# Attention over a sparse graph on one core: gathered rows in a ring, one reduction for a tile's weighted sum, VectorE in the order of the program

## The chip, the cores and the metric

The kernel runs on one core of a Trainium2 chip. A core has five engines that run side by side, each with its own queue of instructions: TensorE (PE, matrix products), VectorE (DVE, elementwise operations and reductions), ScalarE (ACT, functions and copies), GpSimd (POOL, here above all the issuer of indirect DMAs) and SyncE (SP, an issuer of plain DMAs). Engines wait for one another through semaphores; transfers are made by 16 DMA engines. Each of the 128 partitions of on-chip memory (SBUF) holds one row of a tile; results of TensorE land in PSUM, eight banks of 512 float32 values a partition. The metric is the time of one execution on the device, in microseconds (us).

## The reference

There are 3327 nodes with 256 values each, and an adjacency matrix in which an entry is set with probability 0.0024 and the diagonal always. Four layers follow one another: an attention block, a layer that averages over neighbours, and two more attention blocks.

```python
def attention_block(x, adj, w_qkv, w_proj, b_proj, w1, b1, w2, b2, g1, be1, g2, be2):
    qkv = layer_norm(x, g1, be1) @ w_qkv          # 8 heads of 32
    q, k, v = ...
    scores = jnp.einsum('nhd,mhd->hnm', q, k) * SCALE
    scores = jnp.where(adj != 0, scores, -jnp.inf)
    attn = jax.nn.softmax(scores, axis=-1)
    out = jnp.einsum('hnm,mhd->nhd', attn, v).reshape(n, DIM)
    x = x + out @ w_proj + b_proj
    h2 = layer_norm(x, g2, be2)
    return x + jax.nn.gelu(h2 @ w1 + b1) @ w2 + b2    # 256 -> 1024 -> 256

def averaging(x, adj, Wt, bt, Wa, ba, Wp, bp, gamma, beta):
    h = x @ Wt.T + bt                              # 64 values
    s = leaky_relu(h @ Wa.T + ba, 0.2)
    w = softmax(where(adj > 0, s, NEG), axis=1)
    y = x + (w @ h) @ Wp.T + bp
    return layer_norm(y, gamma, beta)
```

## The kernel before

The first stage reads the adjacency matrix once and makes for each node a list of its neighbours, at most 24. Nodes are sorted by the number of neighbours and divided into 26 tiles of 128, a node to a partition. `ROOM[t]` is the number of neighbour rows that tile t needs: 24, 14, 12, 12, 11, 11, 10, 10, then 9 four times, down to 4; together 228. The normalised rows are multiplied with the key, value and query weights, and keys and values go to a table in device memory, 512 values a row.

An attention block (`block`, L634) processes the tiles from the last to the first, so that lists grow from 4 rows to 24, in groups of 2, 2, 3, 4, 4, 4, 3, 2, 1 and 1 tiles (`GROUPS`, L62). For each tile:

- `scores` (L551) loads the tile's own key, value, query row (and, in blocks 0 and 1, the residual x) into `own`: in block 0 by an indirect DMA of POOL (L559), in block 1 and 2 by SP (L564, L566). ACT copies x out of it (L568) and the query into a PSUM bank named `qs` (L571; two such banks). `gather` (L546) issues one indirect DMA on POOL for each neighbour index; it fetches 128 rows of 512 values. Four of them fill a unit; the pool has ten units. For the own row and each unit, VectorE multiplies the keys with the query in place (L576) and sums over each head's 32 values into the scores in PSUM (L577). Then empty places are pushed away (L591), the maximum is subtracted (L593, L595), and ACT takes the exponent (L596).
- `weighed` (L599), one tile later, divides by the sum (L605 to L607), multiplies the values with the weights (L610), and adds the units up: full units onto the first (L622), the partial one (L626), then halves onto halves (L630) and the own row last (L631).
- When a group is complete, `project` (L651 to L665) transposes the result and multiplies it with the projection's weights; the bias is a small matmul for each tile (`bias`, L187). Later steps of the loop (`run`, L720) add the residual and sum it up on the way (`add`, L667, VectorE's L671), normalise (`norm`, L205: squares on ACT, then a chain of some twelve tiny VectorE operations with `root`, L192), turn and feed forward (`feed_forward`: L685, the gelu on ACT at L688, the second matmul with result `f2` at L695), add again, and hand the rows on: block 0 to the averages (`into_averages`, L792), block 1 to the keys of block 2 (`into_keys`, L755), block 2 to the output by indirect DMAs (L711). A group's stages are held in the list `later`, each with the step from which it may run.

The order in which engines carry out their instructions is not the order in which the code emits them: the framework's scheduler lists all instructions of a stage and orders each engine by its own model of costs and by priorities, within what data and buffers allow. Only where `tc.manual_schedule(engines={...})` is entered does the named engine keep the order of the program; before, that is so for VectorE in a part of the adjacency stage only.

The averaging layer (`averaging`, L850) takes its buffers for turned adjacency (`at`) and for rows (`st4`) from the same pool of units.

Of the kernel before, what the change touches and what calls it, by code (L numbers as in the profile page):

```python
# [19 lines left out]
BF = mybir.dt.bfloat16  # L20
# [11 lines left out]
P = 128  # L32
CW = 512
# [26 lines left out]
UNIT = 4  # L60
UNITS = 10
# [20 lines left out]
def chunk_width(c):  # L82
    return min(CW, NP - c * CW)


class Sparse:
# [100 lines left out]
    def bias(self, y, i):  # L187

        self.nc.tensor.matmul(y, self.ones3, self.biases[:, i, :], start=True, stop=False)
# [15 lines left out]
    def norm(self, pool, tiles, sums):  # L205
# [6 lines left out]
        for i, t in enumerate(tiles):  # L212
            xh = pool.tile([P, DIM], F32, tag="xh", name="xh", bufs=2)
            nc.scalar.activation(xh, t, AF.Square, bias=m[:, i : i + 1], accum_out=v[:, i : i + 1])
        nc.vector.tensor_scalar(v[:, :n], v[:, :n], 1.0 / DIM, EPS, ALU.mult, ALU.add)
# [23 lines left out]
    def turned(self, pool, pp, tiles, gamma=None, beta=None, small=None, sums=None):  # L239
# [3 lines left out]
        if sums is not None:  # L243
            rstd, shift = self.norm(pool, tiles, sums)
        elif gamma is not None:
            _, rstd, shift = self.stats(pool, tiles, small)
# [297 lines left out]

    def gather(self, out, table, t, j, held):
# [6 lines left out]
    def scores(self, pool, pp, layer, t, held):  # L552

# [3 lines left out]
        own = pool.tile([P, 4 * DIM], F32, tag="own", name="own", bufs=3)  # L557
        if layer == 0:
# [3 lines left out]
            )  # L562
        elif layer == 1:
            self.after(nc.sync.dma_start(out=own, in_=self.sorted[ts(t, P), :]), self.turning)  # L564
        else:
            nc.sync.dma_start(out=own[:, : 3 * DIM], in_=self.own[t])  # L566
        if layer < 2:
            nc.scalar.copy(self.x[t], own[:, 3 * DIM :])  # L568
# [3 lines left out]
        s = bank[:, ds(DIM, (SLOTS + 1) * HEADS)].rearrange("p (j h) -> p j h", h=HEADS)  # L572
        units = []

        def dot(at, k, n):
            nc.vector.tensor_mul(k, k, query.unsqueeze(1).to_broadcast([P, n, DIM]))  # L576
            nc.vector.tensor_reduce(  # L577
                s[:, ds(at, n), :].rearrange("p j h -> p (j h)"), k.rearrange("p j (h d) -> p j h d", d=HD), AX.X,
                ALU.add,
            )  # L580

        dot(0, own[:, :DIM].unsqueeze(1), 1)
        for j0 in range(0, J, UNIT):
            n = min(UNIT, J - j0)
            u = self.units.tile([P, UNIT, 2 * DIM], F32, tag="unit", name="unit")
            for j in range(n):
                self.gather(u[:, j, :], self.places[layer], t, j0 + j, held)
            dot(1 + j0, u[:, :n, :DIM], n)
            units.append((u, j0, n))
        away = self.away[:, t, :J].unsqueeze(2).to_broadcast([P, J, HEADS])  # L590
        nc.vector.tensor_add(s[:, ds(1, J), :], s[:, ds(1, J), :], away)  # L591
        top = pool.tile([P, HEADS], F32, tag="top", name="top", bufs=3)
        nc.vector.tensor_reduce(top, s[:, : J + 1, :].rearrange("p j h -> p h j"), AX.X, ALU.max)  # L593
        wide = [P, J + 1, HEADS]
        nc.vector.tensor_sub(s[:, : J + 1, :], s[:, : J + 1, :], top.unsqueeze(1).to_broadcast(wide))  # L595
        nc.scalar.activation(s[:, : J + 1, :], s[:, : J + 1, :], AF.Exp)  # L596
        return own, s, units

    def weighed(self, pool, t, own, s, units):  # L599
# [3 lines left out]
        wide = [P, J + 1, HEADS]  # L603
        total = pool.tile([P, HEADS], F32, tag="total", name="total", bufs=3)
        nc.vector.tensor_reduce(total, s[:, : J + 1, :].rearrange("p j h -> p h j"), AX.X, ALU.add)  # L605
        nc.vector.reciprocal(total, total)
        nc.vector.tensor_mul(s[:, : J + 1, :], s[:, : J + 1, :], total.unsqueeze(1).to_broadcast(wide))  # L607

        def weigh(to, v, at, n):
# [971 lines left out]
```

## Time and profile before

| | |
|---|---|
| median of three runs | 2087.87 us (2083.0 to 2097.82) |
| the profiled execution | 2096.42 us |
| its span | 2094.6 us |
| granted clock of TensorE, mean | 0.77 |

| stage | from to, us | VectorE busy | TensorE busy |
|---|---|---|---|
| adjacency, neighbour lists, keys and values | 0 to 306 | | |
| attention block 0 | 306 to 850 | 367.0 | 311.2 |
| averaging | 850 to 1072 | 106.2 | 194.7 |
| attention block 1 | 1072 to 1604 | 356.5 | 367.2 |
| attention block 2 | 1604 to 2094 | 344.1 | 283.3 |

The span is the time from the first to the last instruction in the trace, all numbers in it are of one execution. A group of the profile reads: line, engine, operation, out<-in with their shapes, count, then busy time and mean of one, then the time for which the engine stood idle before them and what ended it. A wait reads: engine, the name and line of the instruction that waited, the instruction it waited for, then us in total, times, and the longest. A line of the timeline reads: start, duration, engine, line, operation; a count behind it, as x2, means that so many instructions are taken together. Waits are inferred from semaphores; busy time counts what overlaps on one engine once.

### The profile page before, as it was taken

What the parts mean: (1) busy time and instruction counts of PE and PEld (TensorE: products, weight loads), DVE (VectorE), ACT (ScalarE), POOL (GpSimd) and SP (SyncE); (2) the same over time, 40 slices, a digit from 0 to 9 for tenths busy, and PEclk for the clock granted to TensorE, in tenths of its full rate; (3) what the DMA queues carried; (4) which work ended last, traced back from release to release, by engine and by line L of the source; (5) the groups of instructions that cost most, each with busy time, mean ns of one, the idle gap of its engine ahead of it and who ended that gap; (6) DMA issues with size and microseconds to landing.
All of it is one profiled execution on the core that took longest, in us unless ns stands there. A gap on an engine that the chain in (4) does not pass through costs nothing. (4 is left out here: it accounts for less than half of the span.)

```text
span 2094.6 us, 17222 instructions
## 1 busy us (share of the span) xinstructions
PE 1263.4 (60%) x4806; PEld 812.1 (39%) x4806; DVE 1342.0 (64%) x3407; ACT 684.9 (33%) x1420; POOL 1001.0 (48%) x946
## 2 busy tenths in 40 slices
PE   3244411556755579699934688567695277655676
PEld 1122200344424337577512454343473154323445
DVE  3567635577776785165636789776732679976871
ACT  3555501233321224122322444334343133322232
POOL 3768757555555531101156645555203666565521
PEclk8667655677767769799976888798798587767778
DMA  8878827555555550858486656656215665565520
GB/s 191 330 300 326 284 79 213 160 163 154 170 148 175 147 131 23 198 154 230 160 284 205 216 166 209 220 178 193 61 56 201 210 186 176 176 190 160 152 65 20
DMA packets 169409, 369.73 MB, mean 177 GB/s; under 512 B 78821, under 2 KB 90291, under 8 KB 165976
## 3 DMA queue, kind: packets, MB, share of 16 engines
q0 software_dynamic: 68624, 222.01, 35.4%
q1 hardware_dynamic: 85689, 112.44, 17.1%
q10 hardware_dynamic: 14990, 34.08, 5.0%
q8 instruction: 40, 0.66, 0.1%
q14 instruction: 66, 0.54, 0.1%
HBM read 279.77 MB, written 77.59 MB: 171 GB/s over the span
## 5 line engine op out<-in xcount | busy, mean ns | idle before, releaser
L546 POOL DMA_INDIRECT unit<-kv,ids x684 | 667.2, 975 | 434.7 <-issue 189.1
L685 PE MATMUL f<-hT,w 128*128 128x256 f32 (+3 forms) x960 | 342.1, 517 | 58.6 <-ACT gT L688 23.2
L256 PE MATMUL tr<-ident,xh 128*128 128x128 f32 x312 | 80.6, 384 | 442.7 <-ACT xh L251 395.6
L695 PE MATMUL f<-w,gT 128*128 128x256 f32 x1248 | 306.4, 399 | 17.9 <-ACT gT L688 14.3
L685 PEld LDWEIGHTS f<-hT,w 128*128 128x128 f32 x960 | 190.4, 219 | 202.6 <-issue 106.0
L695 PEld LDWEIGHTS f<-w,gT 128*128 128x128 f32 x1248 | 238.3, 197 | 68.7 <-ACT gT L688 18.3
L256 PEld LDWEIGHTS tr<-ident,xh 128*128 128x128 f32 x312 | 41.7, 179 | 483.3 <-ACT xh L251 414.8
L576 DVE TENSOR_TENSOR unit<-unit,qs 128x1024 f32<-128x1024 f32 (+3 forms) x198 | 211.7, 1069 | 26.4 <-DMA unit<-kv,ids 15.0
L577 DVE TENSOR_REDUCE qs<-unit 128x32 f32<-128x1024 f32 (+3 forms) x198 | 212.7, 1074 | 4.8 <-DVE qs L607 1.7
L610 DVE TENSOR_TENSOR unit<-unit,qs 128x1024 f32<-128x1024 f32 (+3 forms) x198 | 210.0, 1065 | 0.0
L315 POOL TENSOR_TENSOR m<-a,place 128x3328 f16<-128x3328 fp8e4 x26 | 159.4, 6132 | 78.7 <-ACT a L313 78.6
L688 ACT ACTIVATE gT<-f,b 128x256 f32<-128x256 f32 (+3 forms) x240 | 124.8, 536 | 212.5 <-PE f L685 106.6
L538 PE MATMUL kvps<-wqkv,hT 128*128 128x512 f32 x312 | 171.9, 677 | 29.5 <-ACT hT L262 22.5
L326 DVE MAX8 found<-m 128x8 f16<-128x416 f16 x208 | 111.5, 579 | 39.7 <-POOL m L315 33.1
L664 PE MATMUL proj<-wproj,oT 128*128 128x256 f32 x312 | 109.3, 489 | 42.7 <-ACT oT L659 22.8
L576 DVE TENSOR_TENSOR own<-own,qs 128x256 f32<-128x256 f32 x78 | 32.3, 415 | 141.5 <-ACT qs L571 124.2
L658 PE MATMUL otr<-ident,o 128*128 128x128 f32 x156 | 25.5, 289 | 142.4 <-DVE qs L577 87.4
L990 POOL DMA_INDIRECT sorted<-st,to x26 | 24.8, 955 | 178.7 <-ACT st L542 147.1
L538 PEld LDWEIGHTS kvps<-wqkv,hT 128*128 128x128 f32 x312 | 63.2, 213 | 86.7 <-issue 37.7
L313 ACT ACTIVATE a<-a 128x3328 fp8e4<-128x3328 int32 x26 | 77.3, 2973 | 51.6 <-DMA kv<-st 29.0
L251 ACT ACTIVATE xh<-x,shift,rstd 128x256 f32<-128x256 f32 x104 | 58.4, 594 | 104.5 <-DVE shift L218 80.9
L664 PEld LDWEIGHTS proj<-wproj,oT 128*128 128x128 f32 x312 | 66.9, 235 | 65.6 <-ACT oT L659 28.4
(193 smaller groups left out, 1881.4 us busy)
## 6 DMA issues: line engine op xcount, KB each, us to landing
a<-in_adj SPq DMA_DIRECT2D x25, 1663.5 KB
kv<-st ACTq DMA_DIRECT2D x52, 512.0 KB
own<-sorted SPq DMA_DIRECT2D x26, 512.0 KB
unit<-kv,ids POOLq DMA_INDIRECT x684
adj<-a SPq DMA_DIRECT2D x26, 416.0 KB
own<-qkv SPq DMA_DIRECT2D x26, 384.0 KB
own<-own SPq DMA_DIRECT2D x26, 384.0 KB
w<-in_L_gnn_w SPq DMA_DIRECT2D x6, 1024.0 KB
```

What stands on the lines that cost most here:

```text
L256: nc.tensor.transpose(ps[k][:, ts(q, P)], t[:, ts(k, P)], self.ident)
L315: nc.gpsimd.tensor_mul(m.rearrange("p (s e) -> p s e", e=SEG), a8.rearrange("p (s e) -> p s e", e=SEG), place.unsqueeze(1).to_broadcast([P ...
L326: nc.vector.max(found[:, i, s, :], m[:, ts(s, SEG)])
L538: nc.tensor.matmul(kv, hT[:, k, ts(q, P)], w[:, k, DIM : 3 * DIM], start=k == 0, stop=k == KC - 1)
L546: g = self.nc.gpsimd.indirect_dma_start(out=out, out_offset=None, in_=table, in_offset=bass.IndirectOffsetOnAxis(ap=self.ids[:, t, j : j + ...
L576: nc.vector.tensor_mul(k, k, query.unsqueeze(1).to_broadcast([P, n, DIM]))
L577: nc.vector.tensor_reduce(s[:, ds(at, n), :].rearrange("p j h -> p (j h)"), k.rearrange("p j (h d) -> p j h d", d=HD), AX.X, ALU.add,)
L610: nc.vector.tensor_mul(to.rearrange("p j (h d) -> p j h d", d=HD), v.rearrange("p j (h d) -> p j h d", d=HD), s[:, ds(at, n), :].unsqueeze ...
L664: nc.tensor.matmul(y, oT[:, k, ts(q, P)], wpj[:, k, :], start=False, stop=k == KC - 1)
L685: nc.tensor.matmul(y[:, :w], w1[:, k, ts(f, P)], hT[:, k, :w], start=k == 0, stop=k == KC - 1)
L688: nc.scalar.activation(gT[-1][:, f % 2, :w], y[:, :w], AF.Gelu_apprx_tanh, bias=b1[:, f : f + 1])
L695: nc.tensor.matmul(y, gT[f // 2][:, f % 2, ts(q, P)], w2[:, f, :], start=False, stop=f == FC - 1)
```

## The change

- One tile `ring` of 46 rows takes the place of the ten units of four rows. `take(n)` hands out the next n rows and begins again at the front where they do not fit. A tile takes `ROOM[t]` + 2 rows: the neighbours first, and the tile's own row in the last two, beside them.
- `fetch` is split off `scores`: own row, gathers and the query's copy of a tile are issued after the weighing of the tile two before it, that is a tile ahead of its scores. x no longer passes over ACT; SP writes it by a DMA of its own.
- Products and weighing run over pieces of up to 6 (`PIECE`) and 9 (`WEIGHED`) rows, own row included. The sum over rows is one reduction for a tile that steps from row to row (L656 of the kernel after).
- VectorE keeps the program's order through a whole block.
- `norm` is split in `squares` (residual, sum, ACT's squares) and the rest; what follows waits in the list `middle` and is issued by `between` after the next tile's scores. The averages' preparation is split in the same way (`rest`, a stage of its own).
- The biases of two halves of a bank are one matmul; the flag that ends the accumulation is set once for a bank (`Halves`).

```diff
-UNIT = 4
-UNITS = 10
+RING = 46
+PIECE = 6
+WEIGHED = 9
...
-    def bias(self, y, i):
-        self.nc.tensor.matmul(y, self.ones3, self.biases[:, i, :], start=True, stop=False)
+    def bias(self, ys, q, i):
+        if q % 2 == 0:
+            bank, n = ys.bank(q)
+            self.nc.tensor.matmul(
+                bank[:, : n * DIM], self.ones3, self.biases[:, i, :].unsqueeze(1).to_broadcast([3, n, DIM]),
+                start=True, stop=False,
+            )
...
-    def norm(self, pool, tiles, sums):
+    def squares(self, pool, tiles, sums):
...
             nc.scalar.activation(xh, t, AF.Square, bias=m[:, i : i + 1], accum_out=v[:, i : i + 1])
+        return m, v
+
+    def norm(self, pool, n, m, v):
...
+    def take(self, n):
+        if self.at + n > RING:
+            self.at = 0
+        at = self.at
+        self.at += n
+        return self.ring[:, at : at + n, :]
...
-    def scores(self, pool, pp, layer, t, held):
+    def fetch(self, pp, layer, t, held):
         J = ROOM[t]
-        own = pool.tile([P, 4 * DIM], F32, tag="own", name="own", bufs=3)
+        rows = self.take(J + 2)
+        own = rows[:, J:, :].rearrange("p a b -> p (a b)")
         if layer == 0:
             nc.gpsimd.indirect_dma_start(
...
+            nc.sync.dma_start(out=self.x[t], in_=own[:, 3 * DIM :])
         elif layer == 1:
-            self.after(nc.sync.dma_start(out=own, in_=self.sorted[ts(t, P), :]), self.turning)
+            for to, at in ((own[:, : 3 * DIM], self.sorted[ts(t, P), : 3 * DIM]), (self.x[t], self.sorted[ts(t, P), 3 * DIM :])):
+                self.after(nc.sync.dma_start(out=to, in_=at), self.turning)
         else:
             nc.sync.dma_start(out=own[:, : 3 * DIM], in_=self.own[t])
-        if layer < 2:
-            nc.scalar.copy(self.x[t], own[:, 3 * DIM :])
+        for j in range(J):
+            self.gather(rows[:, j, :], self.places[layer], t, j, held)
         bank = pp.tile([P, CW], F32, tag="qs", name="qs", bufs=2)
         query = bank[:, :DIM]
         nc.scalar.copy(query, own[:, 2 * DIM : 3 * DIM])
+        return rows, bank
+
+    def scores(self, pool, t, rows, bank):
...
-        dot(0, own[:, :DIM].unsqueeze(1), 1)
-        for j0 in range(0, J, UNIT):
-            n = min(UNIT, J - j0)
-            u = self.units.tile([P, UNIT, 2 * DIM], F32, tag="unit", name="unit")
-            for j in range(n):
-                self.gather(u[:, j, :], self.places[layer], t, j0 + j, held)
-            dot(1 + j0, u[:, :n, :DIM], n)
-            units.append((u, j0, n))
+        for lo, w in self.pieces(n, PIECE):
+            k = rows[:, ds(lo, w), :DIM]
+            nc.vector.tensor_mul(k, k, query.unsqueeze(1).to_broadcast([P, w, DIM]))
+            nc.vector.tensor_reduce(
...
-        full = [u for u, _, n in units if n == UNIT]
-        for u in full[1:]:
-            nc.vector.tensor_add(full[0][:, :, DIM:], full[0][:, :, DIM:], u[:, :, DIM:])
...
-        nc.vector.tensor_add(o, o, u[:, 0, DIM:])
+        for lo, w in self.pieces(n, WEIGHED):
+            v = rows[:, ds(lo, w), DIM:].rearrange("p j (h d) -> p j h d", d=HD)
+            nc.vector.tensor_mul(v, v, s[:, ds(lo, w), :].unsqueeze(3).to_broadcast([P, w, HEADS, HD]))
+        o = pool.tile([P, DIM], F32, tag="o", name="o", bufs=5)
+        nc.vector.tensor_reduce(o, rows[:, :n, DIM:].rearrange("p j f -> p f j"), AX.X, ALU.add)
         return o
...
+            def forward(at, group, sums):
+                add_later(at + max(2, len(group)), 1, group, feed_forward(group, sums))
+            def follow(at, group, sums):
+                after, rest = finish(group, sums)
+                if rest:
+                    add_later(at + 1, 2, group, rest)
+                add_later(at + 1 + (len(group) > 2 or rest is not None), 3, group, after)
...
+                    if stage == 0:
+                        middle.append((forward, at, group, squares(group, what)))
+                    elif stage == 1:
...
+                            middle.append((follow, at, group, squares(group, what)))
...
+            with tc.manual_schedule(engines={nc.vector.engine}):
+                waiting, step, outs = None, 0, []
+                got = fetch()
+                for group in [*GROUPS, ()]:
+                    for t in group or (None,):
+                        now = t is not None and (group, t, *self.scores(pool, t, *got))
+                        between()
+                        if waiting:
+                            done, *rest = waiting
+                            outs.append(attended(*rest))
+                        got = fetch()
+                        if waiting and len(outs) == len(done):
+                            add_later(step + 1 + (len(done) > 2), 0, done, project(done, outs))
                             outs = []
+                        waiting = now
+                        run(step)
+                        step += 1
+                between()
+                run(None)
```

## The prediction

> **What bounds the kernel now.** I read the busy shares first, then the span by stage, then VectorE's waits, then the costs of single operations.
>
> ```profile
> PE 1263.4 (60%) x4806; PEld 812.1 (39%) x4806; DVE 1342.0 (64%) x3407; ACT 684.9 (33%) x1420; POOL 1001.0 (48%) x946
> ```
>
> No engine is full on average, so the stages decide. The windows view was asked for the steady middle and the tail of each attention block; its columns are the stretch, its length, then busy time of PE, PEld, DVE, ACT and POOL, the granted clock, DMA share and GB/s.
>
> ```profile
> 322.00:805.00 483.00, 274.44 (x939) 177.02 (x940) 348.24 (x756) 136.77 (x314) 252.91 (x260) 0.71 0.54 156
> 805.00:850.00 45.00, 36.80 (x213) 30.87 (x212) 13.22 (x67) 18.17 (x61) 10.73 (x12) 0.96 0.33 101
> ...
> 1084.00:1529.00 445.00, 299.38 (x957) 181.75 (x958) 341.94 (x751) 165.11 (x359) 229.78 (x233) 0.79 0.58 180
> 1529.00:1604.00 75.00, 67.80 (x300) 47.85 (x298) 13.62 (x81) 40.30 (x106) 9.62 (x10) 1.00 0.33 120
> 1622.00:2048.00 426.00, 251.59 (x825) 157.98 (x826) 335.37 (x711) 118.68 (x245) 235.39 (x239) 0.74 0.54 162
> 2048.00:2094.00 46.00, 31.22 (x172) 26.13 (x170) 4.62 (x27) 12.81 (x35) 5.73 (x6) 0.87 0.07 23
> ```
>
> In the three middles (1354 us together) DVE is the busiest engine: 1025.5 us busy, 328.5 us idle. Matrix work fills the tails. What DVE waits for in the first middle (total us, times, longest):
>
> ```profile
> DVE own L576 <- ACT qs L571: 38.8, 7, 14.8
> DVE total L605 <- ACT qs L596: 21.9, 5, 9.0
> DVE h L818 <- PE hps L810: 14.5, 5, 9.8
> ...
> DVE unit L576 <- DMA unit<-kv,ids: 9.0, 2, 7.7
> ```
>
> The largest is the first product of a tile, behind the copy of its query on ACT, which follows the load of the tile's own row; rows themselves are rarely awaited. So the change moves two quantities: DVE's work, which rises, and its 328.5 us of idling, which it can replace.
>
> **The change, part by part.** The costs come from VectorE's groups by form, and from its timeline in the averaging layer:
>
> ```profile
> L577 DVE TENSOR_REDUCE qs<-unit 128x32 f32<-128x1024 f32 x144 | 175.7, 1220 | 2.2 <-remote 1.6 <-DVE qs L607 0.5
> L576 DVE TENSOR_TENSOR unit<-unit,qs 128x1024 f32<-128x1024 f32 x144 | 174.8, 1214 | 24.4 <-DMA unit<-kv,ids 15.0 <-issue 7.9 <-DVE total L606 1.2
> ...
> L382 DVE TENSOR_REDUCE larger<-more 128x25 bf16<-128x650 f32 x1 | 1.3, 1317 | 0.0
> ...
> L442 DVE TENSOR_REDUCE count<-tops 128x26 f32<-128x624 f32 x1 | 0.8, 793 | 0.0
> ```
> ```profile
> 902.17 0.16 DVE L201 SCALAR_TENSOR_TENSOR nwt<-nwt,rstd 128x4 f32<-128x4 f32 x1
> 902.37 0.16 DVE L202 SCALAR_TENSOR_TENSOR rstd<-nwt,rstd 128x4 f32<-128x4 f32 x1
> ...
> 904.55 0.75 DVE L981 TENSOR_TENSOR st<-st,beta 128x256 f32<-128x256 f32 x2
> ```
>
> 1024 elements take about 1215 ns and 256 elements 415 ns (the same L576 on the own row), so an operation costs 147 ns and 1.04 ns an element. Two independent 417 ns operations of L981 fit in 0.75 us: the second starts 80 ns before the first ends. L202 needs L201's result and starts 40 ns after its end (34 ns by finer times). A pair in dependent order is thus 114 ns dearer than an independent one.
>
> *Products, scores and weighing.* A block has 228 gathered and 26 own rows. Before, 92 operations each for product, score sum and weighing (276); after, pieces of up to 6 and 9 rows make 54 + 54 + 39 = 147. The elements stay; 129 operations fewer save 147 - 80 = 67 ns each: **-8.6 us a block**.
>
> *The sum over neighbours.* Before, 118 contiguous additions (L622, L626, L630, L631) are 78.6 us busy a block, or 69.2 with the 80 ns of overlap taken off each. After, 26 reductions read 254 x 256 = 65,024 elements, each sum stepping over whole rows, 2048 bytes apart. No row of before has that stride. Lower end: contiguous reductions, L442 or L577, 1.04 ns an element, 69.5 us. L382 is the only large reduction with a stride, 100 bytes: (1317 - 147)/650 = 1.80 ns, 118.8 us. Upper end: twice 1.04, a slot lost on every element, 137 us. L382's lines are still packed closer than 2048 bytes, so I take 2.0 ns, near the upper end: 132 us, **+62.6 us a block**.
>
> The Trainium skill, "SBUF — State Buffer", section "Door 1: The DMA port swizzle (why `[64,N]` ≈ `[32,N]`)", says that SBUF is read in 16-byte lines, that full bandwidth needs two hits a line, and that four fp32 is as far as one strides for free. It speaks against this reduction, gives no factor, and would by itself rule out the lower end; L382 agrees, but is one row.
>
> *VectorE in the order of the program.* Before, the framework's scheduler interleaves tiles: in the middles 700, 676 and 655 pairs of neighbours overlap, and only 13, 24 and 9 start as dependent. In the program's order product, score sum and softmax steps follow their own producers: by the two orders 376, 396 and 316 pairs become dependent, x 114 ns = 43 + 45 + 36 = **+124 us for three blocks**. Upper end: all of it. Lower end nothing, if the chip treats wide operations otherwise than L201 and L202.
>
> The Trainium skill, "VectorE: DVE Perf Modes", section "The DRAIN you can't avoid", says that the next operation waits for the pipe anyway and that a semaphore between two costs nothing extra (8 copies in 13.88 us either way). By it these 124 us would be nothing and the sum about 2000; the trace's 0.75 us for two 0.417 us operations contradicts it, and I go by the trace.
>
> DVE's work thus changes by 3 x (62.6 - 8.6) + 124 = **+286 us** (+99 at 1.04 ns, +247 at 1.80, +302 at 2.08).
>
> *Fetch a tile ahead, own row in the ring, query copied at the fetch, norm in two steps.* Own row and query copy are now issued before the weighing of the previous tile is consumed, so L571's wait should go, and the norm's squares on ACT run beside the next tile's scores. That takes away most of the 328.5 us. What comes late next, by the program's fixed order:
> - Groups of two tiles: the second matmul's result f2 is due two steps on. Tile chains of 6 to 10 rows cover 17 to 19 us, while such a feed-forward takes 22 to 26 (squares at 1668.8, last f2 at 1694.7). Behind that wait stand add, squares and the next scores. About 12 us a block.
> - The ring has 46 rows. The three largest tiles (24 + 2, 14 + 2, 12 + 2) overlay the tile but one before, whose rows come free only when its whole sum has ended. Then own row, gathers at 1.25 us each and landing (3.9 us in the chain) come late. About 15 us a block.
> - First gathers and the averages' split step: about 8.
>
> So new waits S of 33 to 37 us a block, some 100 in all, against 328.5: **-228**. Lower bound nothing; upper bound the old waits.
>
> *POOL.* Its gathers start 1.25 us apart:
>
> ```profile
> 1640.64 0.95 POOL L546 DMA_INDIRECT unit<-kv,ids  x1 [0.30 <-issue]
> 1641.89 0.95 POOL L546 DMA_INDIRECT unit<-kv,ids  x1 [0.31 <-issue]
> ```
>
> With own rows (block 0) and scatters that is 350, 317 and 317 us a block, under DVE's about 430 to 470 after, so DVE hides it. If the stride were free, DVE would shrink to about 375 + waits and POOL's order would matter.
>
> *Smaller parts.* One bias matmul for two halves: 52 to 60 fewer small matmuls a block on a PE that has slack in the middles; it counts in the tails. The copy of x moves from ACT to SP's queue: one DMA more per tile in blocks 0 and 1, behind loads of the same queue; ACT, 28 to 37% busy, loses 0.4 us a tile. The x rows are needed only at the projection a tile or more later, so nothing; without that cover some 2 us a tile. Averaging takes the same buffers from the ring: nothing, or a few us either way. In the tails the last groups end sooner because the norm no longer waits its turn among the scheduler's choices: 5 to 8 us each, -20 in all, from the 166 us of the three tails; bounds 0 and -40.
>
> **Sum.** +286 - 228 - 20 = +38. The profiled execution took 2096.42 us, 8.5 above the median 2087.87; the sum is made of the profiled execution's durations and applied to the median: 2126, given as **2125 us** (2134 against the profiled execution).
>
> **Rivals.** (A) The forecast, DVE-bound with a stride near 2 ns: 2085 (1.80 ns, S = 35) to 2165 (2.08 ns, S = 45), chance 0.45.
>
> (B) The fixed order exposes more: each DVE wait now holds everything behind it, where the scheduler could pass another tile's work. For it: L605, L671 and L818 waits on ACT and PE are already there, and PE at .71 to .79 clock is 57 to 67% busy in the middles. Against: products of a later tile stand between most producers and consumers. S = 65 gives +90 more: about 2220, chance 0.12.
>
> (C) **The other side: the stride is nearly free.** For it: L908, 26 elements 392 bytes apart, takes 178 ns against 174 for L443 with 26 contiguous ones. DVE then rises by only 99; cover for f2 shrinks, S about 45. 99 - (328.5 - 135) - 20 = -115: about 1973. With A's waits the sum, at 195 us for each ns an element, turns negative below 1.8 ns and leaves the 1% band below 1.7: from there the stride decides. Chance 0.20.
>
> (D) Stride at L382's price and hardly any waits: +247 - (328.5 - 60) - 20 = -41: about 2045, S = 20. Chance 0.20. It ends on the faster side by one mechanism, the fetch a tile ahead hiding every own row and query.
>
> The rest, 0.03: the fetch doesn't bring rows earlier. Gathers already run up to ten units ahead before, and their order on POOL is still the scheduler's; then the old DMA waits remain with DVE's added work, beyond 2250.
>
> **How the numbers follow.** The likeliest case gives 2125; its own range is 2085 to 2165. 8 times in 10 wants most of A and D and the nearer parts of B and C: **1975 to 2205**. One per cent, about 21 us, is about what a measurement of this kernel can tell from no change. C, nearly all of it below 2067, and most of D give 0.33 faster; A's lower third and D's upper end 0.17 within; the rest of A, B and the remainder 0.50 slower.
>
> **What would show it.** L656's group: 26 x 3 reductions; for 2304 elements (eight neighbours and the own row) 4.8 us at 2.0 ns, 2.5 at 1.04. DVE's busy time: up by some 250 us (286 less 34 ns of gap for each of 1088 pairs). Waits on L571 under a tenth of what they are; new ones on f2 at L697 after groups of two, and on gathers before tiles of 14 and 24 rows. Gathers released by L656 rather than L631. The middles 440 to 490 us each with DVE 85 to 92% busy.
>
> Wrong would be: L656 below 1.4 ns or above 2.5 ns an element; dependent wide operations that overlap after all; S beyond 65 us a block; or the scheduler delaying ACT's or POOL's part so that the fetch ahead isn't one.

## The result

The kernel after takes 2164.11 us (2161.26 to 2166.6), the kernel before beside it 2092.51 us: ratio 1.0347, 95% interval 1.0301 to 1.0393. That is 72 us slower, where 38 were forecast; the two profiled executions, 2163.08 and 2096.42 us, differ by 67. The page of the profile, part 1 (busy time, share, instructions of each engine), of the kernel after:

```profile
PE 1230.6 (57%) x4740; PEld 808.7 (37%) x4740; DVE 1530.5 (71%) x2744; ACT 668.5 (31%) x1366; POOL 976.8 (45%) x946
```

VectorE has 663 instructions fewer and is 188.5 us longer busy. Where the time went is best read in stretches with the same ends in both kernels: from a block's first gather to its last weighing, and from there to the first gather of the next block. The windows view of the kernel before, the three blocks and then the end of block 0 with the averaging layer (stretch, length, busy time of PE, PEld, DVE, ACT, POOL, clock, DMA share, GB/s):

```profile
314.00:792.00 478.00, 263.05 (x878) 167.89 (x879) 338.43 (x732) 133.64 (x308) 259.09 (x266) 0.70 0.56 160
1071.00:1521.00 450.00, 291.38 (x922) 175.41 (x923) 335.00 (x740) 165.78 (x362) 239.52 (x243) 0.78 0.60 186
1609.00:2037.00 428.00, 242.64 (x787) 151.49 (x788) 330.09 (x694) 116.69 (x240) 243.92 (x247) 0.73 0.57 170
792.00:1071.00 279.00, 242.89 (x1376) 174.86 (x1374) 129.72 (x506) 79.64 (x184) 37.95 (x41) 0.93 0.59 169
```

The same of the kernel after:

```profile
312.00:795.00 483.00, 253.20 (x856) 167.41 (x857) 399.57 (x526) 127.70 (x280) 254.00 (x268) 0.71 0.58 170
1103.00:1572.00 469.00, 276.75 (x927) 175.51 (x928) 395.92 (x540) 157.04 (x340) 230.76 (x243) 0.76 0.58 181
1658.00:2102.00 444.00, 225.87 (x768) 147.22 (x769) 387.14 (x487) 117.48 (x238) 235.96 (x247) 0.71 0.54 158
795.00:1103.00 308.00, 251.43 (x1376) 178.29 (x1374) 135.20 (x493) 79.97 (x184) 37.97 (x41) 0.90 0.53 151
```

In the three blocks VectorE's busy time rises from 1003.5 to 1182.6 us (+179), its idle time (length less busy) falls from 352.5 to 213.4 (-139): 40 us in all. The stretch with the averaging layer, in which the change was costed at nothing, takes 29 us more. The rest of the span moves by -2 us.

The new reduction, in VectorE's groups by form:

```profile
L656 DVE TENSOR_REDUCE o<-ring 128x256 f32<-128x2560 f32 x12 | 54.3, 4523 | 0.6
...
L656 DVE TENSOR_REDUCE o<-ring 128x256 f32<-128x6400 f32 x3 | 33.2, 11072 | 0.1
...
L656 DVE TENSOR_REDUCE o<-ring 128x256 f32<-128x1280 f32 x6 | 13.9, 2316 | 0.2
```

From 1280 to 6400 elements the time grows by 8756 ns: 1.71 ns an element at a stride of 2048 bytes, where contiguous elements cost 1.04. What VectorE waits for, from 312 to 2102 us:

```profile
DVE ring L1043 <- PE tf L1042: 98.1, 17, 27.3
DVE ring L621 <- DMA ring<-kv,ids: 67.3, 7, 30.5
DVE x L697 <- PE f L724: 35.0, 6, 9.7
DVE ve L241 <- ACT xh L235: 32.2, 9, 12.0
DVE x L697 <- remote: 24.9, 3, 11.9
...
DVE ring L621 <- ACT qs L607: 10.5, 5, 2.7
```

Of the same list of the kernel before, from 314 to 2037 us:

```profile
DVE own L576 <- ACT qs L571: 124.2, 22, 24.4
...
DVE x L671 <- remote: 20.2, 5, 8.6
...
DVE ve L215 <- issue: 15.4, 5, 8.7
```

The first line of the kernel after is the averaging layer. The wait for the query copy falls from 124.2 us (L576 behind L571) to 10.5 (L621 behind L607); 60 of L621's 67 us for gathered rows are the starts of the three blocks. "Issue" means that the engine waited for nothing that the profile shows, "remote" that the profile can't find what released it; both become important below.

### The profile page after: what moved, and what is told of

It reads as the page before. It is cut to its first block, busy times and chain, and to the rows that moved or that the text cites. A ratio compares the mean times of both kernels' runs of the same rounds, so it can differ in the third digit from the quotient of the medians.

```text
span 2161.3 us, 16464 instructions
## 1 busy us (share of the span) xinstructions
PE 1230.6 (57%) x4740; PEld 808.7 (37%) x4740; DVE 1530.5 (71%) x2744; ACT 668.5 (31%) x1366; POOL 976.8 (45%) x946
## 5 line engine op out<-in xcount | busy, mean ns | idle before, releaser
L580 POOL DMA_INDIRECT ring<-kv,ids x684 | 647.4, 946 | 485.1 <-issue 204.9
L656 DVE TENSOR_REDUCE o<-ring 128x256 f32<-128x1792 f32 (+9 forms) x78 | 343.9, 4409 | 3.3
L621 DVE TENSOR_TENSOR ring<-ring,qs 128x1280 f32<-128x1280 f32 (+3 forms) x162 | 227.5, 1404 | 99.4 <-DMA ring<-kv,ids 67.3
L724 PE MATMUL f<-w,gT 128*128 128x256 f32 x1248 | 288.1, 388 | 8.1 <-issue 7.0
L622 DVE TENSOR_REDUCE qs<-ring 128x40 f32<-128x1280 f32 (+3 forms) x162 | 229.3, 1416 | 9.5 <-issue 4.0
L654 DVE TENSOR_TENSOR ring<-ring,qs 128x1280 f32<-128x1280 f32 (+4 forms) x117 | 217.8, 1888 | 5.3 <-DVE qs L651 1.5
L1059 POOL DMA_INDIRECT sorted<-ring,to x26 | 24.8, 954 | 204.2 <-ACT ring L568 171.2
L631 ACT ACTIVATE qs<-qs 128x56 f32<-128x56 f32 (+9 forms) x78 | 17.2, 220 | 280.8 <-DVE qs L630 100.1
L697 DVE SCALAR_TENSOR_TENSOR x<-f,x 128x256 f32<-128x256 f32 x78 | 29.1, 418 | 92.1 <-PE f L724 60.5
L1013 PE MATMUL ups<-ring,parts 128*128 128x256 fp8e4 (+1 forms) x676 | 84.7, 288 | 15.9 <-DMA ring<-adj 15.9
```

The lines of the kernel that those rows point to most:

```text
L580: g = self.nc.gpsimd.indirect_dma_start(out=out, out_offset=None, in_=table, in_offset=bass.IndirectOffsetOnAxis(ap=self.ids[:, t, j : j + ...
L622: nc.vector.tensor_reduce(s[:, ds(lo, w), :].rearrange("p j h -> p (j h)"), k.rearrange("p j (h d) -> p j h d", d=HD), AX.X, ALU.add,)
L654: nc.vector.tensor_mul(v, v, s[:, ds(lo, w), :].unsqueeze(3).to_broadcast([P, w, HEADS, HD]))
L656: nc.vector.tensor_reduce(o, rows[:, :n, DIM:].rearrange("p j f -> p f j"), AX.X, ALU.add)
L724: nc.tensor.matmul(y, gT[f // 2][:, f % 2, ts(q, P)], w2[:, f, :], start=False, stop=f == FC - 1 and ys.ends(q))
```

## The experiments

Runs made together shared a chip. The kernel before took 2079 to 2093 us in some groups of runs and 1909 to 1912 us in two others, so each run is read against the kernel before in its own group; "slow chip" and "quick chip" below name these two conditions. Whether they are two kinds of chips isn't shown: the record gives the same number, 2, to the chip of one quick group and of the last slow one, so it may be one chip at different times.

### Rows of its own for the averaging layer (slow chip)

```diff
-at = self.take(4)...
+at = self.ring[:, ds(next(first) % 4 * 4, 4), :]...
-both = self.take(4)...
+both = self.ring[:, ds(16 + next(second) % 7 * 4, 4), :]...
```

> Only the averaging layer differs from the kernel after: its turned adjacency (at) always takes rows 0 to 15 of the ring and its node rows (st4) rows 16 to 43, each in turn, so that no at overlays an st4. Theory: the 22 us that the averaging layer lost come from the ring's fixed order, in which every second at overlays node rows that are free only after their store; with rows of its own the waits of the sums' matmul on DMA (15.9 us) go, and the time falls by 15 to 24 us from 2164, to 2140 to 2149. Rival: the transfers themselves are late because the DMA engines are shared; then the time stays within 2160 to 2168.

Measured: 2138.39 us; before on that chip 2081.92, ratio 1.030 (1.022 to 1.038). The ratios alone don't settle 20 us; the stretch does. TensorE's waits between 878 and 1078 us of the kernel after:

```profile
PE ups L1013 <- DMA ring<-adj: 15.9, 3, 5.9
PE tf L1042 <- DVE ring L1043: 2.2, 1, 2.2
```

In the kernel before, as in this experiment, that first line doesn't exist. The stretch from last weighing to first gather, in the windows view of the experiment:

```profile
796.00:1085.00 289.00, 245.02 (x1375) 174.79 (x1373) 135.05 (x493) 80.07 (x184) 37.98 (x41) 0.92 0.58 169
```

308 us became 289, against 279 before: 19 of the 29 us come from the ring's fixed order. An iteration takes rows for two `at` and two `st4`; in a ring of eleven places the second `at` takes the place of an `st4` of three iterations ago, and must wait until its rows have been stored. SyncE's queue, which issues the transposes, names these stores (L1006, 925 to 1010 us of the kernel after):

```profile
SPq L1006 <- DMA sorted<-ring,to: 40.2, 3, 28.1
```

The transpose for the second `at` of the fourth iteration is issued at 933.5 us, when such a store has just landed, and TensorE, free since 943.2, starts on it at 948.5. In the kernel before, both transposes of that iteration wait for TensorE's reads and older transfers only. Later ones wait for stores there too, but are let go 20 to 29 us before TensorE comes to them, so TensorE doesn't wait. About 10 us of the stretch stay unexplained.

### Contiguous additions in place of the strided reduction (slow chip)

```diff
-nc.vector.tensor_reduce(o, rows[:, :n, DIM:].rearrange("p j f -> p f j"), AX.X, ALU.add)
+v = rows[:, :n, DIM:]
+while n > 2:
+    h = n // 2
+    nc.vector.tensor_add(v[:, :h], v[:, :h], v[:, ds(n - h, h)])
+    n -= h
+nc.vector.tensor_add(o, v[:, 0], v[:, 1])
```

> The one reduction of a tile's weighted rows (L656, 114.6 us a block) is replaced by contiguous additions in place, halves onto halves: 94 additions a block over 228 rows of 256 values, 94 x 0.147 + 58,368 x 1.042 ns = 74.6 us, and some 3 us of dependent starts. Theory (VectorE's chain sets the blocks): 36 us less work a block, 108 in all, of which a tenth to a third turns into new waits: 2060 to 2095. Rival (GpSimd's gathers or TensorE would refill the time): 2130 to 2165.

Measured: 2152.5 us, ratio 1.0346 (1.0268 to 1.0424): the rival's number, on this chip. The blocks of the profiled execution, which at 2165.66 us was the slowest of the four:

```profile
315.00:807.00 492.00, 251.20 (x860) 167.82 (x861) 365.14 (x591) 128.12 (x282) 263.27 (x268) 0.71 0.57 167
1115.00:1602.00 487.00, 289.59 (x929) 181.28 (x930) 361.45 (x604) 158.64 (x342) 239.81 (x243) 0.75 0.56 174
1683.00:2110.00 427.00, 223.24 (x771) 145.58 (x772) 352.79 (x551) 117.67 (x240) 245.74 (x247) 0.74 0.56 164
```

VectorE is 103 us less busy than in the kernel after and 113 us longer idle; the second block even grew by 18 us. VectorE alone seemed not to be the bound.

### VectorE's order left to the scheduler (slow chips)

```diff
-with tc.manual_schedule(engines={nc.vector.engine}):
+if True:
```

> The kernel after with VectorE's order in the blocks left to the scheduler; all else stays. Theory: the program's order costs 160 us in gaps between operations (overlaps of 164 us became 37, and 35 us of dependent starts came), and the fetch ahead and the split norm, which stay, are what took the waits away: the gaps close, a part of the waits comes back, 2060 to 2130. Rival: it is the order itself that took the waits away; without it they return in full, 2165 to 2250.

Measured: 2151.64 us, ratio 1.0366 (1.0294 to 1.0437), between the two expectations. The same kernel on two more chips:

> The kernel after with VectorE's order in the blocks left to the scheduler, again. Theory, where the kernel before takes 1912 us and the kernel after 2082: on the slower chip this edit took the dependent starts from 1020 to 99 and the gaps by 108 us, but 31 + 17 + 20 us of waits and 30 us of longer ends of blocks came; without that chip's stalls fewer waits come, 40 to 80 us are gained: 2000 to 2045. Where the kernel before takes 2090: 2145 to 2160. Rival (order costs nothing by itself, or the waits take it all): within 15 us of the kernel after.

> The kernel after with VectorE's order in the blocks left to the scheduler, once more. Where the kernel before takes 2080, 2130 to 2150 as twice before. Where it takes 1910 and the kernel after 2082: theory, the gaps shrink by 108 us and 30 us of longer ends of blocks and 20 to 40 us of waits come: 2010 to 2045. Rival: 2070 to 2090, the order is worth nothing by itself.

Measured: 2136.78 us (1.029, 1.0205 to 1.0375) and 2137.55 us (1.0293, 1.0191 to 1.0394), both on slow chips. None of the three ratios is clear of the 1.0347 of the kernel after; the stretches of the traces differ more clearly. The blocks of the last run:

```profile
313.00:786.00 473.00, 230.15 (x811) 153.92 (x812) 371.51 (x521) 125.42 (x275) 255.15 (x268) 0.70 0.59 174
1097.00:1542.00 445.00, 266.92 (x865) 167.60 (x866) 365.58 (x523) 148.91 (x327) 231.24 (x243) 0.76 0.61 190
1640.00:2071.00 431.00, 218.59 (x726) 142.20 (x727) 362.05 (x482) 116.26 (x234) 236.58 (x247) 0.71 0.56 162
```

They take 1349 us (1352 in the other two) against 1396 of the kernel after; from last weighings to what follows it is 21 us more (28 in the other two). So the order costs about 45 us in the blocks, and gives back half at their ends, where the matrix work of the last groups stands. For a quick chip this isn't shown: all three fell on slow ones.

### Products of a tile ahead of its score sums (slow chips)

```diff
 nc.vector.tensor_mul(k, k, query.unsqueeze(1).to_broadcast([P, w, DIM]))
+for lo, w in self.pieces(n, PIECE):
+    k = rows[:, ds(lo, w), :DIM]
     nc.vector.tensor_reduce(
```

> In the kernel after a tile's products (L621) are all issued before its score sums (L622), in place of product, sum, product, sum. 50 sums a block then stand behind an instruction that they do not need. Theory (a dependent neighbour costs 114 ns more than an independent one): 50 x 0.114 = 5.7 us a block, 17 us in all, of which 12 to 17 are seen: 2147 to 2152. Rival (a wait between two operations of one engine costs nothing): 2161 to 2167, with the same gaps in the trace.

> All products of a tile ahead of its score sums, again. On the slower chip the dependent starts fell by 26 a block only, the gaps by 3 us a block, and more was lost in waits for gathered rows. Theory: where the kernel before takes 1912 us, 3 us a block less of gaps and up to 6 us more of waits at the first rows: 2075 to 2090, no gain, as a tile's last rows are needed earlier. Rival (each separated pair gains 114 ns on the chain): 2062 to 2070.

Measured: 2172.95 us (1.0454, 1.0381 to 1.0526) and 2166.77 us (1.0459, 1.0371 to 1.0546): no gain, rather a loss. In the first run, gaps and overlaps between neighbours improve by 3 us a block, as 26 and not 50 pairs a block became independent: 115 ns for each, which is the price that was forecast. The waits of L621 for rows rise by 4 us a block (67.3 to 79.8 in all), presumably because a tile's last rows are needed earlier. Three microseconds a block are easily lost again.

### The norm in one piece; the fetch not ahead (quick chip, kernel before 1909.14 us)

The first edit issues what waits in `middle` at once:

```diff
-if now is None:
-    between()
+between()
```

> The kernel after with the norm in one piece again: what was put off until after the next tile's scores (turning, feed forward, the next layer's products) follows at once behind the squares. Theory: VectorE then waits for ScalarE's squares in place, some 3 to 4 us for each of 10 groups, once a block and twice in block 1, 30 x 2 us net as the second matmul's results also come one tile's scores earlier: 2175 to 2225. Rival: that earlier start is worth more than the squares cost, since VectorE waits 53 us for those results (L697) in the three blocks: 2130 to 2160.

The second moves `got = fetch()` from behind the weighing to the line before `scores`:

> The kernel after with a tile's fetch (own row, gathers, query copy) put in the code right before its scores, not a tile ahead. Theory: GpSimd's and ScalarE's order is the scheduler's, and a gather starts when its ring rows come free, wherever the code has it: within 2150 to 2180. Rival: the place in the code sets the priorities, and without the tile ahead the waits of the first product return (131 us in the kernel before): 2200 to 2290.

Measured: 2115.6 us (ratio 1.1059, 1.1017 to 1.1101) and 2083.24 us (1.0897, 1.0863 to 1.0931). The expectations were written for the slow chip, where the kernel after took 2164 us. On a quick chip it takes 2082.53 us where the kernel before takes 1912.31 (below). Beside that, the norm in one piece costs 33 us. VectorE's waits for the squares, in this run and in the kernel after on a quick chip:

```profile
DVE ve L241 <- ACT xh L235: 106.6, 38, 12.0
...
DVE ve L241 <- ACT xh L235: 47.2, 11, 12.0
```

And the place of the fetch in the code is worth nothing: in both places GpSimd's gathers stand idle for 132 us until a tile's sum (L656) has freed rows of the ring, and VectorE waits for rows as long (68.5 and 69.0 us).

### A longer way to the feed forward's use; half of the gathers (the same quick chip)

```diff
-add_later(at + max(2, len(group)), 1, group, feed_forward(group, sums))
+add_later(at + max(3, len(group)), 1, group, feed_forward(group, sums))
```

> The kernel with contiguous additions (2152 us, where 105 us less work on VectorE became 106 us more waiting) and one edit: the result of a group's feed forward is taken up at least three tiles later, not two. Theory 1 (the fixed distance in tiles, with TensorE's feed forward behind it, sets the blocks): the waits for that result, 93 us in three blocks, go for the most part: 2070 to 2115. Theory 2 (ring rows and GpSimd's gathers set them): the same time shows up as waits of L621 for gathered rows: 2135 to 2155.

```diff
-self.gather(rows[:, j, :], self.places[layer], t, j, held)
+if layer == 0 or j % 2 == 0:
+    self.gather(rows[:, j, :], self.places[layer], t, j, held)
```

> The kernel with contiguous additions, in which the second and third attention block gather only every other neighbour row; the rows left out hold what lay in the ring, so the output isn't the reference's. The first block is unchanged and serves for comparison. Theory 1 (the feed forward's distance sets the blocks): the stretches from first product to last weighing of the second and third block, 474 and 418 us, fall only by the waits for gathered rows in them, to 440 to 460 and 400 to 410. Theory 2 (gathers set them): VectorE's own work remains, to 390 to 410 and 370 to 385; in all 2152 falls to 2040 to 2075.

Measured: 2002.44 us (1.048, 1.0445 to 1.0515) and 1992.88 us (1.0425, 1.0394 to 1.0457). Both expectations took 2152 us as the start and missed the chip. Beside contiguous additions alone (2008.8 us in the other quick group, below), the longer way is worth some 7 us, and half of the gathers some 16. In the halved blocks VectorE's busy time stays, GpSimd's falls by 43%, and the stretches of blocks 1 and 2 hardly move:

```profile
1044.00:1465.00 421.00, 275.60 (x929) 176.24 (x930) 360.99 (x605) 157.96 (x342) 135.83 (x135) 0.78 0.41 134
1546.00:1941.00 395.00, 220.86 (x769) 145.60 (x770) 352.01 (x550) 117.88 (x240) 141.56 (x139) 0.74 0.35 105
```

With all gathers these two are 424 and 403 us. With contiguous additions on a quick chip, then, gathers don't set the blocks, and the feed forward's distance hardly does.

### Before, after and contiguous additions on one quick chip

> The kernel before, for a profile beside the others: it took 2082 to 2093 us on one chip and 1909 us on another. Theory: the slower chip adds stalls in which an engine waits for nothing that the profile shows, or for a releaser that it can't name (259 us of such idle time, named remote, over all engines in the first profile); on the faster chip these rows are near zero, VectorE's busy time is the same, and its idle time in the three blocks is 339 us less some 180, about 160. Rival: operations themselves are faster there: the same idle time, shorter rows.

> The kernel after, beside the kernel before on this chip. Theory: VectorE's chain, some 200 us longer than before, is what sets the blocks, and the waits that it replaced were for a good part stalls of the slower chip; so where the kernel before takes 1909 us, this takes 2075 to 2100 (ratio 1.085 to 1.10), and where it takes 2090, 2155 to 2170. Rival: fetching ahead in the code is what cost the earlier runs their time, and this kernel stays 80 us above the 2083 us of the kernel that fetches late: 2150 to 2170 where that took 2083.

> Contiguous additions in place of the strided reduction, again. Theory: where the kernel before takes 1909 us, nothing but VectorE's chain is in the way and the 108 us of work come off in full: 75 to 108 us below the kernel after on the same chip. Where it takes 2090, 0 to 20 us below. Rival: the step distance of the feed forward eats the gain on both chips: 0 to 30 below on either.

> Contiguous additions and at least three tiles from a feed forward to its use. Theory: on the faster chip the longer distance gains little, within 15 us of contiguous additions alone; on the slower one the waits for that result (93 us) are for a part stalls which a longer distance hides: 20 to 60 us below. Rival: the distance of two tiles was the bound: 40 to 80 us below on either.

Measured, beside 1912.31 us of the kernel before: after 2082.53 us (ratio 1.0903, 1.0842 to 1.0964), contiguous additions 2008.8 (1.0508, 1.045 to 1.0566), these with the longer way 2002.22 (1.0479, 1.0423 to 1.0535). The theories on the profile, the kernel after and the longer way held; that on contiguous additions, 75 to 108 us, is missed by 1 us. The change costs 170 us here, not 72, and the 103 us of VectorE's work that the slow chip had turned into waits come off by 74. The blocks of the kernel before on this chip:

```profile
312.00:730.00 418.00, 249.03 (x878) 161.63 (x879) 337.43 (x732) 133.78 (x307) 260.76 (x266) 0.74 0.63 183
1013.00:1402.00 389.00, 275.12 (x924) 171.12 (x925) 334.18 (x741) 164.99 (x362) 240.12 (x243) 0.81 0.68 215
1490.00:1852.00 362.00, 230.51 (x784) 146.12 (x785) 327.60 (x694) 117.08 (x240) 244.56 (x247) 0.75 0.67 200
```

and of the kernel after:

```profile
315.00:756.00 441.00, 239.98 (x856) 161.31 (x857) 399.54 (x526) 128.03 (x280) 253.63 (x268) 0.72 0.63 187
1062.00:1510.00 448.00, 273.41 (x927) 174.54 (x928) 395.63 (x540) 158.03 (x340) 230.66 (x243) 0.78 0.60 189
1596.00:2022.00 426.00, 223.18 (x766) 146.02 (x767) 386.90 (x486) 117.69 (x238) 236.02 (x247) 0.72 0.56 164
```

Busy times of VectorE agree with those of the slow chip to within 0.8%. Its idle time in the blocks doesn't: 170 us before (352 on the slow chip) and 133 after (213). Of the slow chip's, 118 us before and 79 after stand under "issue" and "remote"; on the quick chip nothing does. Waits with a named cause are shorter there too, as that for the query copy, 124.2 us on the slow chip:

```profile
DVE own L576 <- ACT qs L571: 76.6, 21, 27.1
```

What differs can be seen in one place, the first norm of block 0 in the kernel after, on the slow chip (timeline: start, duration, engine, line, operation, idle time before it and releaser):

```profile
358.57 0.16 DVE L241 TENSOR_SCALAR ve<-ve 128x2 f32<-128x2 f32 x1
360.93 0.17 DVE L218 TENSOR_SCALAR rstd<-ve 128x2 int32<-128x2 int32 x1 [2.21 <-issue]
...
363.07 0.16 DVE L222 SCALAR_TENSOR_TENSOR nwt<-nwt,rstd 128x2 f32<-128x2 f32 x1 [1.28 <-issue]
364.50 0.21 DVE L223 SCALAR_TENSOR_TENSOR rstd<-nwt,rstd 128x2 f32<-128x2 f32 x1 [1.27 <-issue]
...
375.74 0.22 DVE L651 TENSOR_TENSOR qs<-qs,total 128x48 f32<-128x48 f32 x1 [1.89 <-remote]
```

and on the quick one:

```profile
360.87 0.21 DVE L241 TENSOR_SCALAR ve<-ve 128x2 f32<-128x2 f32 x1
361.12 0.17 DVE L218 TENSOR_SCALAR rstd<-ve 128x2 int32<-128x2 int32 x1
...
361.52 0.16 DVE L222 SCALAR_TENSOR_TENSOR nwt<-nwt,rstd 128x2 f32<-128x2 f32 x1
361.71 0.16 DVE L223 SCALAR_TENSOR_TENSOR rstd<-nwt,rstd 128x2 f32<-128x2 f32 x1
...
363.11 0.22 DVE L651 TENSOR_TENSOR qs<-qs,total 128x48 f32<-128x48 f32 x1
```

From L241 to L651 it takes 17.2 us on the one and 2.2 on the other, with the same durations. The 15 us between are stalls, for most of which the profile has no cause. On the quick chip the releaser "remote" doesn't occur in the waits of these two kernels; on the slow chip it holds some 260 us of waits of all engines in the kernel before and 91 in the kernel after. What the slow chips' engines wait for was not found. TensorE's granted clock differs a little as well, 0.77 on the slow and 0.79 on the quick chip in the kernel before, and its busy time in the three blocks is 797 and 755 us; whether that is a cause or goes along with the stalls isn't shown.

### All three at once: contiguous additions, rows of its own, the scheduler's order (slow chips)

> Contiguous additions, rows of its own for the averaging layer's at and st4, and VectorE's order left to the scheduler, all on the kernel after. Theory: 74 us (additions), 19 (averaging) and 40 to 80 (order) add up, as VectorE's chain holds all but the averaging layer: where the kernel before takes 1912 us, 1910 to 1950, no better than it. Rival: with the order free and less to do, the waits that VectorE had hidden take over: 1965 to 2000; or the ring's larger operations and earlier rows show: below 1900.

> As the kernel with contiguous additions, rows of its own for the averaging layer and the scheduler's order, and with at least three tiles from a feed forward to its use. Theory: the scheduler already places the use where its model has the result ready, so the distance in the code matters little: within 10 us of that kernel. Rival: the priorities follow the code, and waits for TensorE (L697) fall: 10 to 30 us below.

> Contiguous additions, rows of its own for the averaging layer, the scheduler's order, once more. Where the kernel before takes 2080, 2085 to 2105. Where it takes 1910: theory, 74 and 19 us off what the kernel with the order free takes, less some waits for the feed forward (L702, 147 us on the stalling chip): 1930 to 1970, still slower than before, because its larger operations do not make up for its longer ends of blocks. Rival: at or below 1905.

Measured: 2092.47 us (ratio 1.0081, 1.0041 to 1.0121), with the longer way 2088.89 (1.0088, 1.0047 to 1.013), and on another slow chip 2095.71 (1.0097, 1.0049 to 1.0145). The number given for a slow chip (2085 to 2105) held, and so did the theory that the longer way is within 10 us. These are the best of the variants on slow chips, and still slower than the kernel before by just under 1%. Undoing the three parts thus takes the ratio from 1.0347 to 1.0081, some 55 of the 72 us; the remaining 17 are not attributed. No version was found that beats the kernel before; on a quick chip this one was not seen.

## Why the prediction was right or wrong

The direction was right, the size wrong: 72 us against 38. Two terms of the sum failed on the forecast's own chip: the waits, put at -228 us, gave -170, and tails and averaging, put at -20, gave +27. The third, VectorE's work, put at +286, gave +210, and this miss hid most of the other two. (Work and waits are counted here as the forecast did, with the short gaps behind dependent operations, 31 us, as work: +179 and -139 as busy and idle time.)

So that the time lay in the range, and inside case A's band (2164 of 2165), is luck. The direction is, too: the forecast's own sum, with the stride that was measured (1.71 ns), gives -19 us, faster. The band isn't what A's terms give either: with 1.80 ns and S = 35 they come to 2091, with 2.08 ns and S = 45 to 2176.

**VectorE's work (+286 forecast).** As busy time this was "some 250 us"; measured +179 and, on the quick chip, +183. The mechanism held, the stride's price did not: 1.71 ns, not 2.0, so three blocks' sums cost 344 us, 57 less than the 401 they were costed at. That one row, L382 at 1.80, was nearer than the reasoning that moved away from it. The Trainium skill, "SBUF — State Buffer", section "Door 1: The DMA port swizzle (why `[64,N]` ≈ `[32,N]`)", was right that such a stride isn't free. The runs give its factor in this case, 1.71/1.04 = 1.64.

**The order (+124 forecast).** Between the first product and the last weighing of each block on the quick chip, the durations of VectorE's instructions, summed, rise by only 45 us. Overlaps between neighbours fall from 175 to 38 us, and gaps of under 0.3 us rise from 3 to 37: 171 us. On the slow chip the two make 157. Forecast were 124 and, within the 67 ns of each saved operation, 31 of lost overlap: 155. As VectorE's time that step held. What it costs the kernel is less: with the order free on slow chips, 104 us of gaps and overlaps came back and the blocks shortened by 47. The Trainium skill, "VectorE: DVE Perf Modes", section "The DRAIN you can't avoid", says of eight copies that the semaphore between them costs nothing extra; that doesn't carry over to this case, where 1055 pairs stand with a gap, 35 ns on average, and 56 did before.

**The waits (-228 forecast).** As idle time measured -139 on the slow chip, -37 on the quick one. (With the 34 ns gaps counted as idle the forecast said -191.) The step that failed is a reading: the idle time of the kernel before was taken as the kernel's own, "328.5 us of idling, which it can replace". About half of it, 183 of 352 us, is absent on the quick chip. The rows said so for a good part: 118 us of VectorE's waits in the blocks stood under "remote" and "issue", where nothing in the code is named that an edit could move, and 79 of them are still there in the kernel after. The new waits, forecast at some 100 us in three blocks, are 146 on the slow chip (gaps over 0.3 us from first product to last weighing). Without the 79 they are 67, as on the quick chip (65.6, 19 to 27 a block). So the new waits that have a cause in the code were put too high, and the stalls that stay were put at nothing.

**Tails (-20) and averaging ("nothing, or a few us either way").** This step failed as well. In the blocks the sum was +58 and the trace shows +40; outside it was -20 and the trace shows +27. Of these 47 us of error, 19 are the averaging layer's rows, shown by giving it its own, some 10 more in the same stretch are unexplained, and the rest is the gain at the ends of the blocks, which didn't come. Why it didn't stays open: VectorE's fixed order doesn't explain it, as without it the ends took 21 to 28 us longer. Rows from a pool and rows from a ring had been taken as the same, ten places of four against eleven; what counts is which earlier row a place follows.

**Rivals.** B, new waits of 65 us a block from the fixed order, did not come: some 49 on the slow chip, stalls included, and 22 on the quick one. The split norm helps to keep them off, worth 33 us on a quick chip. C fell with 1.71 ns. D was nearest in the stride and had the wrong waits on this chip. "The fetch doesn't bring rows earlier" was right in its mechanism, as moving the fetch changes nothing (2083 and 2082.5 us), but not in its price: the wait for the query copy fell just as far without it (L621 behind L607: 24.5 us with the late fetch, 23.5 without). That GpSimd's gathers are hidden held on a quick chip: half of them gone moved little.

## What to carry to other kernels

Before idle time is counted as a gain, divide it by what ended it: waits without a releaser in the code can't be counted on to go, and may belong to the chip that was profiled; here even named waits were shorter on a quick one. A ring that hands out places in order is not a pool with as many buffers: look at which place each buffer follows, and when that one comes free. An engine's fixed order is paid in each pair of neighbours that need one another; with some thousand pairs that took more of VectorE's time (171 us) than the expensive reduction added (108 us).

## What was not expected of the hardware

The same program takes 1912 us in one group of runs and 2092 in another, with durations of VectorE's instructions that agree (in the kernel after, L656 at 2560 elements: 4526 and 4523 ns). Where VectorE could be compared, the difference is stalls of about 1 to 4 us between small instructions. Where they occur they also hide work: 103 us less on VectorE were worth 0 to 12 us there (ratios 1.0346 and 1.0347, medians 2152 and 2164) and 74 us without them. What causes them stays open, and so does whether they belong to a chip or to a time.
